# A two-dimensional convolution with Toeplitz blocks, followed by a score-weighted sum: X in two layouts, and the second convolution with the Toeplitz blocks as weights

## The chip, the cores and the metric

The kernel runs on one core of one Trainium2 chip. The metric is device time in microseconds (us) of one execution, the median of several runs. A profile is one further execution, recorded by the hardware profiler; its times are us from the start of its span. The engines are named as the profile does: PE (TensorE matmuls), PEld (TensorE weight loads), DVE (VectorE), ACT (ScalarE), POOL (GpSimd) and SP (SyncE, which here only issues DMAs).

## What is computed

The input x has 4 images, 64 channels, 256 x 256 pixels, in f32. Two layers follow each other. Cut to what matters:

```python
# layer 0: per channel c, a causal 2-D convolution with a separable kernel, and a bias
hx, hy = implicit_filter(X...), implicit_filter(Y...)      # [256, 64] each, three small sine layers
k = hx[:, None, :] * hy[None, :, :]                        # per channel an outer product
y = irfft2(rfft2(x, 512) * rfft2(k, 512) / 512)[..., :256, :256]
x = y + x * bias[:, None, None]
# layer 1: per image and channel
scores = einsum('bpsd,bptd->bpst', x, x) / sqrt(256)
red = sum(scores * weights, axis=-1, keepdims=True)        # weights: [64, 256, 256]
x = batch_norm(x + red)                                    # mean and variance per channel
```

As the kernel k is an outer product, the convolution of a channel is two one-dimensional convolutions, each a product with a lower triangular Toeplitz matrix of 256 x 256: `y = Tx X Ty'`.

## The kernel before

**Channels.** Everything is done channel by channel, 64 of them, four images (two pairs v and u) at a time. The 128 partitions hold two halves of 64 rows, so all products are 64 x 64 tiles, and four of them (t = 0 to 3: two halves of the input partitions, two of the output partitions) stand in the program one after the other. I call such four a group. Each f32 product leaves two matmul records and two weight loads in the trace.

**The products of one channel**, with the columns that each group moves:

- The first convolution, `z_slots` (line 263), in two halves m = 0, 1 of 8 groups: 256, 128, 64, 64 columns and the same again. Blocks of X are the weights, Toeplitz blocks move. A part that two output blocks share is made once from the sums `xs` (`sums`, line 225, on DVE) by `shared_slots` (line 234): 4 groups of 64 columns; ACT copies it to `kept` (line 243). ACT and DVE bring the result to SBUF as z (`copy_z`, line 272; `add_shared`, line 278).
- The second convolution, `x0_slots` (line 329), in two halves m of 8 groups: 256, 192, 128, 64 columns and the same again. Blocks of z are the weights, Toeplitz blocks move. `add_bias` (line 350) takes each half out of PSUM on DVE, adds bias times x from `xt`, and writes x0.
- The scores, `gram` (line 398), in two halves v of 8 groups: four of 192 columns and four of 128. DVE multiplies them with the weights (`weigh_pair`: lines 435 and 424).

That is 52 groups and 7,424 columns for a channel: 2,560 in the second convolution, 2,048 in the first, 256 shared, 2,560 for the scores.

**The rest of layer 1.** POOL adds the weighted scores over partitions (`all_sum`, line 489), DVE adds the sum to x0 (`add_red`, line 505), ACT squares and writes the normalised output (`squares`, line 558; `finish`, line 622).

**Order.** The order on each engine is written out by hand in the loop over channels. Iteration c does the second convolution of channel c, the first convolution of channel c + 1, the scores of channel c, and later steps of channels c - 1 to c - 4. On PE: `x0_slots(c, m=0)` with two `shared` groups; `x0_slots(c, m=1)` alternating with `z_slots(c+1, m=0)`; `z_slots(c+1, m=1)`; `gram(c, 0)`; `gram(c, 1)` with the first two `shared` groups of channel c + 2. On DVE: `add_bias` m=0, `sums(c+2)`, `add_red` of channel c - 2 first half, `add_bias` m=1, `add_red` second half, `add_shared` twice, then the eight small products and two large ones of `weigh_pair`, twice.

**PSUM.** One pool `ps` of 4 tiles, two banks each, filled in turn; a tile is reused when the fourth one before it has been read.

**DMAs.** SP issues, for each channel, four loads of `xt` (256 KB each, channel c + 3), four of the Toeplitz tile `toep` (16 of its 64 partitions each, channel c + 3) and four stores `out`. ACT issues the load of the weights `w` and a small store `rows`. `toep` is copied to the other 64 partitions by ACT (`copy_h`, line 208). Channel 0 has its own order: `first_x0` (line 366) does the first two blocks of both halves before the last two.

Of the kernel before, what the change touches and what calls it, by code (L numbers as in the profile page):

```python
# [16 lines left out]
P = 128  # L17
EMB = 33
FFT = 2 * S
H = P // 2  # L20
# [21 lines left out]
def conv_scores_bn_kernel(  # L42
    ctx: ExitStack,
    tc: tile.TileContext,
    xT: bass.AP,
    wl: bass.AP,
    zw: bass.AP,
# [21 lines left out]

    xts, ws, hs = {}, {}, {}  # L70

    def load_xt(c, v, n):
        if c not in xts:
            xts[c] = ld.tile([P, 2, 4, S], F32, tag="xt", name=f"xt_{c}", bufs=4)
        part = bass.ts(n, 2)
        nc.sync.dma_start(xts[c][:, v, part], xT[c, v, :, part])

    PARTS = ((0, 0), (1, 0), (0, 1), (1, 1))
# [28 lines left out]
    for part in PARTS:  # L107
        load_xt(0, *part)
    eye_sb = const.tile([P, P], F32, name="eye_sb")
# [4 lines left out]
    for part in PARTS:  # L114
        load_xt(1, *part)
    g_sb = const.tile([P, 2 * S + H], F32, name="g_sb")
# [99 lines left out]
    def pair_of_banks(name):  # L216
        return ps.tile([P, 2, 2, S], F32, tag="ps", name=name)
# [4 lines left out]
    def sums(c):  # L222

        xss[c] = wk.tile([P, 2, S], F32, tag="xs", name=f"xs_{c}")
        nc.vector.tensor_tensor(xss[c], xts[c][:, :, 1], xts[c][:, :, 2], ALU.add)

# [21 lines left out]
    def z_slots(c, m, p1):  # L248


        toep = hs[c].rearrange("p (b s) -> p b s", s=H)
        for k in range(2):
            for i, (cols, outs) in enumerate((
                (slice(9, 13), slice(0, 4)),
                (slice(5, 13, 7), slice(0, 3, 2)),
                (slice(7, 8), slice(1, 2)),
                (slice(12, 13), slice(0, 1)),
            )):
                for t in range(4):
                    u, v = t % 2, t // 2  # L260
                    rows = bass.ts(u, H)
                    out = p1[bass.ts(v, H), u, k].rearrange("p (b s) -> p b s", s=H)
                    nc.tensor.matmul(  # L263
                        out[:, outs], lhsT=xts[c][rows, v, i, bass.ts(2 * m + k, H)],
                        rhs=toep[rows, cols], start=(i == 0), stop=(i == 3),
                    )
                yield

    def copy_z(c, m, p1):
        z = zs[c][:, m].rearrange("p u k s -> p (u k) s")  # L270
        y = p1.rearrange("p u k s -> p (u k) s")
        nc.scalar.copy(z[:, :, :P], y[:, :, : P - 1 : -1])  # L272

    def add_shared(c, m, p1):
        z = zs[c][:, m].rearrange("p u k (b s) -> p (u k) b s", s=H)
        y = p1.rearrange("p u k (b s) -> p (u k) b s", s=H)
        part = kept[c][:, m].rearrange("p u (k s) -> p (u k) s", s=H)
        nc.vector.tensor_tensor(  # L278
            z[:, :, :1:-1, ::-1], y[:, :, :2],
            part[:, :, None, :].to_broadcast([P, 4, 2, H]), ALU.add,  # L280
        )

    def plain_slots(c, m, p1):


        toep = hs[c][:, PLAIN:]
        for k in range(2):
            for i in range(4):
                for t in range(4):
                    u, v = t % 2, t // 2  # L290
                    rows = bass.ts(u, H)
                    nc.tensor.matmul(  # L292
                        p1[bass.ts(v, H), u, k, : S - H * i],
                        lhsT=xts[c][rows, v, i, bass.ts(2 * m + k, H)],
                        rhs=toep[rows, H * i : S], start=(i == 0), stop=(i == 3),
                    )
                yield
# [6 lines left out]
    def take(*slots):  # L304

        slots = list(slots)
        while slots:
            slots = [s for s in slots if next(s, s) is None]

    def take_with(slots, between):  # L310

        for n, _ in enumerate(slots):
            if n % 4 == 3:
                next(between, None)

    def copy_z_plain(c, m, p1):
        for u in range(2):
            nc.scalar.copy(zs[c][:, m, u], p1[:, u, :, ::-1])

    def x0_slots(c, z, m, p2):  # L320


        toep = hs[c]
        for i in range(2):
            for k in range(4):
                for t in range(4):
                    v, u = t % 2, t // 2
                    rows = bass.ts(v, H)
                    nc.tensor.matmul(  # L329
                        p2[bass.ts(u, H), v, i, : S - H * k],  # L330
                        lhsT=z[rows, k // 2, u, k % 2, bass.ts(2 * m + i, H)],
                        rhs=toep[rows, H * k : S], start=(k == 0), stop=(k == 3),
                    )
                yield

# [5 lines left out]
    def add_bias(c, m, p2, split=False):  # L341
        part = bass.ts(m, 2)
        if split:
            for v in range(2):
                nc.vector.scalar_tensor_tensor(  # L345
                    st8[c][0][:, v, part], xts[c][:, v, part], chan_sb[:, 0, c : c + 1],
                    p2[:, v, :, ::-1], ALU.mult, ALU.add,
                )
            return
        nc.vector.scalar_tensor_tensor(  # L350
            st8[c][0][:, :, part], xts[c][:, :, part], chan_sb[:, 0, c : c + 1],
            p2[:, :, :, ::-1], ALU.mult, ALU.add,
        )

    def first_x0(z):

        toep = hs[0]
        p2 = [pair_of_banks(f"p2_0_{m}") for m in range(2)]
        for half in range(2):
            for m in range(2):  # L360
                for i in range(2):
                    for k in range(2 * half, 2 * half + 2):
                        for t in range(4):
                            v, u = t % 2, t // 2
                            rows = bass.ts(v, H)
                            nc.tensor.matmul(
                                p2[m][bass.ts(u, H), v, i, : S - H * k],
                                lhsT=z[rows, k // 2, u, k % 2, bass.ts(2 * m + i, H)],
                                rhs=toep[rows, H * k : S],
                                start=(i == 0 and k == 0), stop=(i == 1 and k == 3),  # L370
                            )
                if half:
                    add_bias(0, m, p2[m], split=True)

# [432 lines left out]
    for part in PARTS:  # L807
        load_xt(2, *part)
    for n in range(4):
# [4 lines left out]
    def begin_z(c):  # L814
        zs[c] = wk.tile([P, 2, 2, 2, S], F32, tag="z", name=f"z_{c}")

# [20 lines left out]
    for c in range(C - 2):  # L837
# [5 lines left out]
        if f >= 0:  # L843
            tot = sum_squares(f, moms[f])
        parts_of(c, 0)
        if c + 3 < C:
            load_xt(c + 3, 0, 0)
        if c:
            p2 = pair_of_banks(f"p2_{c}_0")
            take_with(x0_slots(c, z, 0, p2), shared)  # L850
            if short:
                keep_shared(c + 1, both)
            keep_rows(p)
            load_w(c + 1, nc.scalar)
            add_rows(p)
            add_bias(c, 0, p2)
        else:
            load_w(c + 1)
            first_x0(z)
        if q >= 0:  # L860
# [4 lines left out]
        else:  # L865
            steps = iter(())
        parts_of(c, 1)
        if c + 3 < C:
            load_xt(c + 3, 1, 0)
            for n in range(2):  # L870
                load_h(c + 3, n)
# [5 lines left out]
        next(steps, None)  # L877
        slots = []
        if c:
            p2 = pair_of_banks(f"p2_{c}_1")  # L880
            slots.append(x0_slots(c, z, 1, p2))
        p1 = [pair_of_banks(f"p1_{c + 1}_0")]
        slots.append((z_slots if short else plain_slots)(c + 1, 0, p1[0]))
        take(*slots)
        copy_any = copy_z if short else copy_z_plain
        copy_any(c + 1, 0, p1[0])
        if c:
            add_bias(c, 1, p2)
        next(steps, None)
        parts_of(c, 2)  # L890
        if c + 3 < C:
            load_xt(c + 3, 0, 1)
            for n in range(2, 4):
                load_h(c + 3, n)
# [15 lines left out]
        if q >= 0:  # L910
            minus_mean(moms[q])
            squares(q, moms[q], 0)
        parts_of(c, 3)
        if c + 3 < C:
            load_xt(c + 3, 1, 1)
        if q >= 0:
            squares(q, moms[q], 1)
        parts_of(c, 4)
        gram(c, 0)
        shared = iter(())  # L920
        if c + 2 < C - 1:
            both = ps.tile([P, 2, 8, H], F32, tag="ps", name=f"shared_{c + 2}")
            shared = shared_slots(c + 2, both)
        gs = gram_banks(c, 1)
        take_with(gram_slots(c, 1, gs), shared)
        weigh_pair(c, 1, gs)
    last_channels(C - 1)
# [71 lines left out]
```

## Time and profile before

| | before |
|---|---|
| median of 3 runs | 900.13 us (898.49 to 902.55) |
| the profiled execution | 892.19 us, of which its span is 890.4 us |
| granted TensorE clock, mean over the span | 0.993 |
| PE, PEld, DVE, ACT, POOL busy | 96%, 90%, 81%, 70%, 54% |
| matmul records | 26,626, and as many weight loads |
| DMA | 175.56 MB, mean 197 GB/s |

A busy PE in this table is matmul records laid side by side; four tiles run at once, so a record's length is not the time that it takes from the others. In the groups of instructions, `L329 PE MATMUL p<-toep,z 64*64 64x256` is a matmul of line 329, 64 x 64 weights, 256 columns moved, which writes a PSUM tile p from toep and z; `xCOUNT` stands after it, then busy us, and the mean ns of one.

### The profile page before, as it was taken

The page shows a single profiled execution, that of the slowest core. Times are in us where ns is not written, and L with a number is a line of the kernel's source. Part 1 is how long each engine was busy: PE and PEld are TensorE (multiplying, and loading weights), DVE is VectorE, ACT ScalarE, POOL GpSimd, SP SyncE. Part 2 cuts the span into 40 slices and gives each one's busy share as a digit, 9 for nine tenths or more (in the row PEclk, how much of TensorE's full clock was granted, in tenths as well). Part 3 has the DMA queues.
Part 4 walks back from the last instruction along what each step waited for, and adds up shares of the span by engine and source line. Part 5 has one row for each costly group of instructions (what it writes and reads, how often), then busy time and mean ns, then how long its engine had stood idle before and what let it go on. Part 6 is the DMA issues. An engine that isn't in the chain of part 4 may idle for free.

```text
span 890.4 us, 59137 instructions
## 1 busy us (share of the span) xinstructions
PE 857.6 (96%) x26626; PEld 800.0 (90%) x26626; DVE 721.2 (81%) x2160; ACT 621.9 (70%) x1157; POOL 480.8 (54%) x255
## 2 busy tenths in 40 slices
PE   7999999999999998999999999999999999999994
PEld 5899999899899897989899899898999899998984
DVE  3478888888788787888788888888788788888887
ACT  2237778677677676767778677667677668767687
POOL 0065565566465565565565565565565566566440
PEclk9999999999999999999999999999999999999997
DMA  6634666666566665666666666666666666666535
GB/s 194 212 123 135 215 210 209 199 210 208 190 193 219 196 216 184 205 208 197 209 199 211 208 195 198 212 204 202 193 216 197 197 214 196 226 204 200 169 125 191
DMA packets 103545, 175.56 MB, mean 197 GB/s; under 512 B 24219, under 2 KB 25148, under 8 KB 103292
## 3 DMA queue, kind: packets, MB, share of 16 engines
q1 hardware_dynamic: 80188, 149.66, 49.9%
q10 hardware_dynamic: 18224, 21.85, 8.3%
q8 instruction: 209, 3.42, 1.6%
q0 software_dynamic: 4880, 0.27, 0.7%
q14 instruction: 44, 0.36, 0.1%
HBM read 102.56 MB, written 69.03 MB: 193 GB/s over the span
## 4 chain that ended last, share of the span: by engine, by line
PE 90%; DVE 3%; issue 2%; DMA 2%; ACT 1%; POOL 1%; SPq 0%; ACTq 0%; DVEq 0%
PE g L398 31%; PE p L329 30%; PE p L263 25%; PE shared L234 3%; DMA g_dram<-g_sb 1%; PE p L292 1%; POOL rd L489 1%; DVE junk L435 0%; DMA fw_sb<-in_fw 0%; DMA toep<-g_dram 0%; DVE x L505 0%; DVE x L345 0%; DMA xt<-in_xT 0%; DVE x L547 0%; ACT o L622 0%
## 5 line engine op out<-in xcount | busy, mean ns | idle before, releaser
L329 PE MATMUL p<-toep,z 64*64 64x64 f32 (+3 forms) x8064 | 400.9, 297 | 4.1 <-issue 4.1
L489 POOL PARTITION_ALL_REDUCE rd<-pr x61 | 375.9, 6162 | 26.5 <-DMA pr<-rows 26.3
L263 PE MATMUL p<-toep,xt 64*64 64x64 f32 (+2 forms) x7808 | 337.2, 271 | 6.6 <-issue 6.2
L329 PEld LDWEIGHTS p<-toep,z 64*64 64x64 f32 x8064 | 324.0, 133 | 20.2 <-issue 8.3
L398 PE MATMUL g<-x 64*64 64x128 f32 (+1 forms) x8192 | 311.2, 297 | 3.3 <-issue 2.1
L263 PEld LDWEIGHTS p<-toep,xt 64*64 64x64 f32 x7808 | 284.4, 133 | 27.0 <-issue 12.3
L398 PEld LDWEIGHTS g<-x 64*64 64x64 f32 x8192 | 278.4, 133 | 16.3 <-issue 7.5
L350 DVE SCALAR_TENSOR_TENSOR x<-xt,chan_sb,p 128x1024 f32<-128x1024 f32 x122 | 156.2, 1280 | 77.8 <-PE p L329 77.6
L622 ACT ACTIVATE o<-x,sh,g 128x512 f32<-128x512 f32 x252 | 201.7, 803 | 0.3 <-DVE sh L610 0.3
L435 DVE SCALAR_TENSOR_TENSOR junk<-g,w 128x192 f32<-128x192 f32 x512 | 152.4, 354 | 48.8 <-PE g L398 48.0
L479 POOL DMA_DIRECT2D pr<-rows x61 | 54.2, 888 | 217.0 <-DMA rows<-across 139.7
L505 DVE SCALAR_TENSOR_TENSOR x<-x,rd 128x1024 f32<-128x1024 f32 x122 | 148.6, 1219 | 7.0 <-ACT rd L498 6.8
L558 ACT ACTIVATE sq<-x,mom 128x1024 f32<-128x1024 f32 x127 | 145.0, 1142 | 2.1
L243 ACT COPY kept<-shared 128x512 f32<-128x512 f32 x61 | 35.8, 586 | 116.4 <-PE shared L234 116.4
L234 PE MATMUL shared<-toep,xs 64*64 64x64 f32 x1952 | 106.2, 218 | 0.2 <-issue 0.2
L272 ACT COPY z<-p 128x512 f32<-128x512 f32 x122 | 71.4, 586 | 44.3 <-PE p L263 43.0
L511 POOL PARTITION_ALL_REDUCE mom<-mom x62 | 24.2, 391 | 139.9 <-DVE x L505 137.0
L234 PEld LDWEIGHTS shared<-toep,xs 64*64 64x64 f32 x1952 | 92.2, 134 | 1.5 <-issue 0.4
L424 DVE SCALAR_TENSOR_TENSOR pr<-g,w 128x512 f32<-128x512 f32 x126 | 84.2, 668 | 0.0
L278 DVE TENSOR_TENSOR z<-p,kept 128x512 f32<-128x512 f32 x122 | 83.1, 682 | 0.8 <-ACT z L272 0.8
L208 ACT COPY toep<-toep 64x832 f32<-64x832 f32 x63 | 55.7, 884 | 12.8 <-DMA toep<-g_dram 11.4
L498 ACT COPY rd<-rd 64x512 f32<-64x512 f32 (+1 forms) x62 | 38.0, 613 | 32.7 <-POOL tot L564 8.4
(100 smaller groups left out, 442.2 us busy)
## 6 DMA issues: line engine op xcount, KB each, us to landing
xt<-in_xT SPq DMA_DIRECT2D x256, 256.0 KB
out<-o SPq DMA_DIRECT2D x256, 256.0 KB
w<-in_wl ACTq DMA_DIRECT2D x61, 320.0 KB
toep<-g_dram SPq DMA_DIRECT2D x252, 52.0 KB
rows<-across ACTq DMA_DIRECT2D x61, 16.0 KB
pr<-rows POOLq DMA_DIRECT2D x61, 4.0 KB, 3.3
w<-in_wl SPq DMA_DIRECT2D x3, 320.0 KB
g_dram<-g_sb ACTq DMA_DIRECT2D x1, 576.0 KB
```

What stands on the lines that cost most here:

```text
L234: nc.tensor.matmul(both[bass.ts(v, H), u, k], lhsT=xss[c][rows, v, bass.ts(k, H)], rhs=toep[rows, 11], start=(k == 0), stop=(k == 3),)
L263: nc.tensor.matmul(out[:, outs], lhsT=xts[c][rows, v, i, bass.ts(2 * m + k, H)], rhs=toep[rows, cols], start=(i == 0), stop=(i == 3),)
L278: nc.vector.tensor_tensor(z[:, :, :1:-1, ::-1], y[:, :, :2], part[:, :, None, :].to_broadcast([P, 4, 2, H]), ALU.add,)
L329: nc.tensor.matmul(p2[bass.ts(u, H), v, i, : S - H * k], lhsT=z[rows, k // 2, u, k % 2, bass.ts(2 * m + i, H)], rhs=toep[rows, H * k : S], ...
L350: nc.vector.scalar_tensor_tensor(st8[c][0][:, :, part], xts[c][:, :, part], chan_sb[:, 0, c : c + 1], p2[:, :, :, ::-1], ALU.mult, ALU.add,)
L398: nc.tensor.matmul(gs[bass.ts(h, H), u, o, :], lhsT=xb[rows, v, i, m, :], rhs=xb[rows, v, i, t, :], start=(i == 0), stop=(i == 3),)
L424: nc.vector.scalar_tensor_tensor(pr[:, 2 * v : 2 * v + 2].rearrange("p u (t s) -> p u t s", s=H), both[:, :, COL, :], 1.0 / math.sqrt(S), ...
L435: nc.vector.scalar_tensor_tensor(junk, g[:, part, :], 1.0 / math.sqrt(S), w[:, 3 * n : 3 * n + 3, :], ALU.mult, ALU.mult, accum_out=red0[: ...
L489: nc.gpsimd.partition_all_reduce(rd[:, part].rearrange("p b s -> p (b s)"), sp[:, part].rearrange("p b s -> p (b s)"), P, RED.add,)
L505: nc.vector.scalar_tensor_tensor(x0[:, v], x0[:, v], 1.0, rd[:, 2 * v, None, :].to_broadcast([P, 4, S]), ALU.mult, ALU.add, accum_out=moms ...
L558: nc.scalar.activation(sq, st8[c][0][:, v], AF.Square, bias=mom[:, 5:6], accum_out=mom[:, 6 + v : 7 + v])
L622: nc.scalar.activation(o, y, AF.Identity, bias=sh, scale=g)
```

## The change

X comes to the chip a second time. `xR` holds it with rows on the partitions, `xT` with columns (and now in reversed order of columns). `xr`, loaded from `xR`, feeds the first convolution and `sums`, so the rows are convolved first; `xt` is only read by `add_bias`. The host swaps the two filters accordingly and reverses one axis of the output again.

In the second convolution weights and moving operand are exchanged: a Toeplitz block of 64 columns is the weight, and z moves, two blocks of 256 columns in one product where two are due. Its groups become 512 and 256 columns for m=0, and 512, 512, 512 and 256 for m=1. To make this possible z is stored as `[P, 4, 2, S]`, and its result comes out of PSUM in forward order.

In the loop the four `shared` groups of channel c + 1 now all stand in `x0_slots(c, m=0)`, two after each of its groups, and two `z_slots` groups stand after each of the four groups of `x0_slots(c, m=1)`. `gram(c, 1)` stands alone. The PSUM tile of `shared` is therefore taken second in the iteration, not before the last. SP issues four more loads a channel: `xt` of channel c + 2 and `xr` of channel c + 3, from 3 buffers each. `first_x0` is gone, and channel 0 is done like the others.

```diff
+    def load_xr(c, v, n):
+        if c not in xrs:
+            xrs[c] = ld.tile([P, 2, 4, S], F32, tag="xr", name=f"xr_{c}", bufs=3)
+        part = bass.ts(n, 2)
+        nc.sync.dma_start(xrs[c][:, v, part], xR[c, v, :, part])
...
     def take_with(slots, between):
 
-        for n, _ in enumerate(slots):
-            if n % 4 == 3:
+        for _ in slots:
+            for _ in range(2):
                 next(between, None)
...
         toep = hs[c]
-        for i in range(2):
-            for k in range(4):
-                for t in range(4):
-                    v, u = t % 2, t // 2
-                    rows = bass.ts(v, H)
-                    nc.tensor.matmul(
-                        p2[bass.ts(u, H), v, i, : S - H * k],
-                        lhsT=z[rows, k // 2, u, k % 2, bass.ts(2 * m + i, H)],
-                        rhs=toep[rows, H * k : S], start=(k == 0), stop=(k == 3),
-                    )
-                yield
+        products = [(0, 2 * m, 2)]
+        if m:
+            products += [(1, 1, 2), (2, 0, 2)]
+        products += [(2 * m + 1, 0, 1)]
+        for k, i, n in products:
+            for t in range(4):
+                v, u = t % 2, t // 2
+                rows = bass.ts(v, H)
+                nc.tensor.matmul(
+                    p2[bass.ts(u, H), v, 2 - n :], lhsT=toep[rows, S - H * (k + 1) :][:, :H],
+                    rhs=z[rows, i : i + n, u], start=(k == 0), stop=(n == 1),
+                )
+            yield
...
-        if c:
-            p2 = pair_of_banks(f"p2_{c}_0")
-            take_with(x0_slots(c, z, 0, p2), shared)
-            if short:
-                keep_shared(c + 1, both)
+        p2 = pair_of_banks(f"p2_{c}_0")
+        shared = iter(())
+        if short:
+            both = ps.tile([P, 2, 8, H], F32, tag="ps", name=f"shared_{c + 1}")
+            shared = shared_slots(c + 1, both)
+        take_with(x0_slots(c, z, 0, p2), shared)
+        if short:
+            keep_shared(c + 1, both)
...
-        slots = []
-        if c:
-            p2 = pair_of_banks(f"p2_{c}_1")
-            slots.append(x0_slots(c, z, 1, p2))
+        p2 = pair_of_banks(f"p2_{c}_1")
         p1 = [pair_of_banks(f"p1_{c + 1}_0")]
-        slots.append((z_slots if short else plain_slots)(c + 1, 0, p1[0]))
-        take(*slots)
+        take_with(x0_slots(c, z, 1, p2), (z_slots if short else plain_slots)(c + 1, 0, p1[0]))
...
+        if c + 2 < C:
+            load_xt(c + 2, 1, 1)
         if c + 3 < C:
-            load_xt(c + 3, 1, 1)
+            load_xr(c + 3, 1, 1)
...
         gram(c, 0)
-        shared = iter(())
-        if c + 2 < C - 1:
-            both = ps.tile([P, 2, 8, H], F32, tag="ps", name=f"shared_{c + 2}")
-            shared = shared_slots(c + 2, both)
-        gs = gram_banks(c, 1)
-        take_with(gram_slots(c, 1, gs), shared)
-        weigh_pair(c, 1, gs)
+        gram(c, 1)
```

At the start SP now loads `xr` of channel 0, the constants, `w`, `xt` of channel 0 and `xr` of channel 1, then the Toeplitz tiles with `xt` of channel 1 and `xr` of channel 2 between them: 2 MB (eight loads of 256 KB) more than before, half of it ahead of the first Toeplitz tile.

## The prediction

> **What bounds the kernel now.** First the busy times and the chain that ended last, to see which engine sets the end.
>
> ```profile
> PE 857.6 (96%) x26626; PEld 800.0 (90%) x26626; DVE 721.2 (81%) x2160; ACT 621.9 (70%) x1157; POOL 480.8 (54%) x255
> PE 90%; DVE 3%; issue 2%; DMA 2%; ACT 1%; POOL 1%; SPq 0%; ACTq 0%; DVEq 0%
> ```
>
> PE has 90% of the chain, so I ask what a channel costs on PE. The chain in order of time shows where each channel's score products begin (start, length):
>
> ```profile
> 46.18 3.42 PE g L398 x85
> ...
> 111.19 3.42 PE g L398 x90
> 123.90 3.42 PE g L398 x90
> 136.61 3.42 PE g L398 x89
> 149.32 3.70 PE g L398 x88
> ...
> 818.01 3.48 PE g L398 x96
> ```
>
> Clean channels follow each other at 12.71 us. From 46.18 to 818.01 lie 58 channels, 13.31 us each. So 0.60 us a channel is lost, 36 us over 61 channels. What is a clean channel made of? Groups of instructions by form, line 329 (behind the first bar: busy us in all, ns of one record):
>
> ```profile
> L329 PE MATMUL p<-toep,z 64*64 64x256 f32 x2016 | 189.5, 379 | 1.0 <-issue 1.0
> L329 PE MATMUL p<-toep,z 64*64 64x64 f32 x2016 | 107.9, 218 | 1.3 <-issue 1.3
> ```
>
> 192 more columns cost 161 ns, 0.839 ns a column and record; two records each, so 7,424 columns need 12.45 us. Only 0.26 us of a clean channel is the price of having 52 groups: 5 ns a group.
>
> And the 0.60 us? I went to one late channel; chain in order of time, 173 to 178 us:
>
> ```profile
> 174.46 0.55 PE p L263 x16
> 175.01 0.92 issue
> 175.93 1.56 PE p L263 x56
> ```
>
> PE waits 0.92 us for nothing that the profile names. In the waits, too, PEld's largest are "issue" (28 us before lines 263, 329 and 398); none for data reaches 4 us in all. The DMA queues show what it is:
>
> ```profile
> q1 hardware_dynamic: 80188, 149.66, 49.9%
> q10 hardware_dynamic: 18224, 21.85, 8.3%
> q8 instruction: 209, 3.42, 1.6%
> ```
>
> q8 moves instructions: 209 packets of 16 KB for 53,252 matmul and weight-load instructions, a block of 256 each. In the packet records every PE gap over 0.25 us between 50 and 840 us falls on the same place of the count of PE instructions modulo 256, about 1.3 us after the block's packet ended. So PE runs out of instructions. From the moment it passes one block's border, the next packet starts 1.33 us later on average, takes 1.10 us (1.6% of 16 engines over the span, by 209), and is usable 1.3 us after that: 3.9 us (5% to 95%: 3.1 to 4.7 us, after 150 us). A block lasts 16 groups: 16 x 12.71 / 52 = 3.91 us. Every other block is late. Setting those latencies against the windows that the order of groups gives, the mean shortfall is 0.17 us a block, 3.25 blocks a channel: 0.56 us, against 0.60 seen. I take this as the cause.
>
> [...]
>
> **The change, part by part,** against the profiled execution's 892.19 us.
>
> *Fewer groups.* 16 groups of the second convolution become 6, with the same 2,560 columns; the program falls from 13,313 to 10,753 matmuls. 10 x 5 ns x 62 channels = -3 us. No row has 512 columns; the records from 64 to 256 columns lie on one line, so I take the line. It could gain nothing or cost a few ns: 0 to -5 us.
>
> *Fewer blocks.* 43,012 instructions are 168 blocks, 2.63 a channel. A block now lasts 16 x 12.66 / 42 = 4.82 us on average, though 8 groups of the first convolution followed by 8 of 192 score columns still last under 3.9. With the latency unchanged the shortfall is 0.05 us a block, 0.13 a channel.
>
> *More loads.* 256 x 256 KB = 67.1 MB. By q1's row (49.9% for 149.66 MB) that is 22 points: the 16 engines go from 60 to 83% busy. A block's packet must find its turn there. Packets asked for while 40 to 60% of the engines were busy in the next us started 1.1 us later, at 80% and more 1.6 us, with single means up to 1.8. I add 0.4 us to the latency (from 0 to 1.0): shortfall 0.13 us a block, 0.35 a channel (0.39 and 1.02 at +1.0). Scaled by 0.60 / 0.56 that is 0.37 instead of 0.60: 0.23 x 61 = -14 us; between -28 us at +0 and +25 us at +1.0.
>
> *SP's queue.* An `xt` issue takes 0.65 us, four more a channel 2.6 us; SP issues 6.5 us of 13.3 now and waits 379 us in all for ACT's outputs, so it has room. But at the fourth place `xr` stands behind `out` and `xt`: 0.45 us of issue and 0.75 us of transfer (256 KB at the 355 GB/s of stretches with all engines busy) later than `xt` today. `sums` on DVE needs it. Today `xs` starts 1.67 us (median) after the last packet and never earlier than 0.63 us, so about 1.0 is spare:
>
> ```profile
> DVE xs L225 <- DMA xt<-in_xT: 8.7, 12, 2.0
> DVE x L350 <- PE p L329: 77.6, 113, 2.4
> DVE junk L435 <- PE g L398: 48.0, 88, 5.9
> ```
>
> 0.2 us of new wait, and as `add_bias` can start 0.4 us sooner (m=0 has 768 columns, not 1,280), 0.6. Behind it in DVE's order stand `add_red`, then `add_bias` m=1, which waits for PE anyhow: the last two rows are 126 us of DVE waiting for PE, 2 us a channel. Priced at nothing under that cover; bare, it is 0.6 x 61 = 37 us.
>
> *PSUM.* With `shared` taken second, the first half of z for channel c + 1 takes the tile of `gram(c-1, 1)`. From the timeline, second convolution's start and last read of that tile:
>
> ```profile
> 409.73 0.39 PE L329 MATMUL p<-toep,z 64*64 64x256 f32 x3
> 411.46 0.65 DVE L424 SCALAR_TENSOR_TENSOR pr<-g,w 128x512 f32<-128x512 f32 x1
> ```
>
> The read ends 2.4 us after; PE comes to it after 768 + 256 + 512 columns, 2.6 us. Zero, but bare only by 0.2 us: 0.1 us late would be 6 us. `add_bias`, `copy_z` and `add_shared` keep their sizes; reversed and forward reads differ by nothing in the rows (1,280 ns for line 350 reversed, 1,219 for line 505 forward, which sums besides), so zero, with 60 ns x 122 = -7 us of DVE at most, off the path. The loads use buffers that an earlier iteration has read; one load of `w` goes from SP to ACT.
>
> *Start.* 1 MB more ahead of the first Toeplitz tile and the store g_dram (14.16 to 20.41 us in the chain, then the load of toep, then PE at 27.19): 1 MB at 355 GB/s is 3 us. The DMA is 0.66 busy before 30 us, so part may hide; the second extra MB delays channel 2's tile. +3 us, 0 to +6. Losing `first_x0` costs nothing: m=0 now needs only z's first half.
>
> Sum: 892.2 - 3 - 14 + 3 = 878 us. The median of the runs lies 7.9 us above the profiled execution; so 886.
>
> **The rivals.**
>
> *The fetching engine fills up (slower).* Each packet of q8 runs on one DMA engine, and if it is always the same, that engine does per channel 96 packets of 2 KB x 96 ns = 9.2, 8 of `w` x 130 ns = 1.0, 2.63 blocks x 1.10 = 2.9, small ones 0.4: 13.5 us by mean durations. That is above 13.31, and loads, `sums` and PE would follow it: 13.5 x 61 against 13.31 is +12, +3 at the start: 907, median 915. By medians (84, 102, 1009 ns) it is 11.9 and doesn't bind; it decides from about 13 us. For it: durations stretch when all engines are busy. Against: before, the same sum is 11.1 of 13.3 and `xs` rarely waits.
>
> *The fetch slows by what the change saves (no change).* At +0.7 us of latency the shortfall is 0.64 a channel, as now: 892 - 3 + 3, median 900.
>
> *The latency stays (more gain).* 892.2 - 3 - 28 + 0 = 861, median 869. For it: packets started after 0.6 us, not 1.5, between 100 and 150 us, at the same DMA share.
>
> *The late `xr`* loses its cover, when its packets queue a us longer: half of 37 us on top of the sum is 896, median 904.
>
> **How the numbers follow.** Forecast 0.42 (own range 876 to 894), fetching engine 0.22, slowed fetch 0.16, unchanged latency 0.12, late `xr` 0.08. A run of this kernel can tell 0.5% from no change, 895.6 to 904.6. Faster: nearly all of the forecast and the unchanged latency, 0.51. Same: most of the slowed fetch, 0.15. Slower 0.34. Range 868 to 914: it leaves out about half of the fetching engine and a little below.
>
> **What would show it.** Right: q8 near 170 packets; line 340 with 512 columns near 379 + 256 x 0.839 = 594 ns; clean channels at 12.65 us; a mean channel near 13.0; PE's issue waits down by a third or more; DMA near 280 GB/s; the score products of channel 0 some 3 us later. Wrong: PE waiting for `xs`, `g` or `xr`; `xs` waiting in most channels; channels of 13.5 us with DMA flat at 9; 512 columns well off the line.

## The result, and the profile after

The changed kernel takes 934.50 us, the median of 4 runs (929.13 to 941.93), where before takes 900.03. The ratio is 1.0386, with an interval of 1.0308 to 1.0463: slower, by 35 us. The profiled execution took 929.13 us, its span 927.4, at a mean granted clock of 0.983 (0.993 before). The clock is not the loss: clean channels take 12.64 us in the changed kernel, and 12.64 in `one_layout` (below), at 0.992.

The page of the changed kernel, busy times and then shares of the chain that ended last:

```profile
PE 862.1 (93%) x21506; PEld 676.6 (73%) x21506; DVE 706.6 (76%) x2158; ACT 614.0 (66%) x1157; POOL 481.3 (52%) x255
DMA 34%; DVE 15%; PE 12%; POOL 11%; ACT 11%; issue 8%; SPq 8%; ACTq 0%; DVEq 0%; POOLq 0%
```

PE is still busy for 93% of the span, but its share of the chain fell from 90% to 12%. A busy time doesn't say who sets the end. One group of instructions by form (busy us, ns of one), and three DMA queues (packets, MB, share of 16 engines):

```profile
L340 PE MATMUL p<-z,toep 64*64 64x512 f32 x2048 | 279.0, 590 | 0.0
q1 hardware_dynamic: 116908, 216.46, 70.2%
q10 hardware_dynamic: 18368, 22.18, 7.5%
q8 instruction: 169, 2.77, 1.3%
```

The 512 columns cost what the line through the shorter products said (590 ns, 594 by the line), and there are 40 instruction blocks fewer (169 packets of q8, 209 before). A clean channel takes 12.64 us, the mean of 58 channels is 13.85 (13.31 before). The waits of the changed kernel say where that goes (first a line of the page, with DVE's idle time before `sums` behind the last bar; then us in all, times, longest):

```profile
L234 DVE TENSOR_TENSOR xs<-xr 128x512 f32<-128x512 f32 x61 | 42.4, 694 | 153.6 <-DMA xr<-in_xR 101.5
DVE xs L234 <- DMA xr<-in_xR: 101.5, 36, 4.8
DVE x L354 <- PE p L340: 11.9, 5, 8.3
DVE x L489 <- ACT rd L482: 14.3, 8, 6.7
POOL rd L473 <- DMA pr<-rows: 65.7, 43, 4.1
PEld g L382 <- DVE x L354: 45.9, 34, 4.1
PE g L382 <- DVE x L354: 34.0, 29, 3.7
```

The scores now wait for `add_bias`, which stands on DVE behind `add_red` and `sums`, and `sums` waits for `xr`. PE's gaps of over 0.1 us between matmul records from 50 to 840 us, counted in the trace, are 40 us: 32 before scores and 8 at borders of instruction blocks (one place of the count of PE instructions, the sequencer's included, modulo 256). Before, they were 13 us, all at block borders. All gaps below are counted in this way.

### The profile page after: what moved, and what is told of

The parts are those of the page before. It is cut to its first block, busy times and chain, and to the rows that moved or that the text cites. A ratio compares the mean times of both kernels' runs of the same rounds, so it can differ in the third digit from the quotient of the medians.

```text
span 927.4 us, 49216 instructions
## 1 busy us (share of the span) xinstructions
PE 862.1 (93%) x21506; PEld 676.6 (73%) x21506; DVE 706.6 (76%) x2158; ACT 614.0 (66%) x1157; POOL 481.3 (52%) x255
## 4 chain that ended last, share of the span: by engine, by line
DMA 34%; DVE 15%; PE 12%; POOL 11%; ACT 11%; issue 8%; SPq 8%; ACTq 0%; DVEq 0%; POOLq 0%
DMA xr<-in_xR 12%; POOL rd L473 10%; DMA pr<-rows 7%; DVE x L489 7%; PE g L382 6%; DMA toep<-g_dram 4%; DMA rows<-across 4%; PE p L340 3%; ACT sq L542 3%; ACT o L606 3%; DMA w<-in_wl 3%; SPq L77 3%; PE p L272 2%; DMA out<-o 2%; SPq L212 2%
## 5 line engine op out<-in xcount | busy, mean ns | idle before, releaser
L340 PE MATMUL p<-z,toep 64*64 64x512 f32 (+1 forms) x3072 | 359.9, 519 | 0.1
L382 PE MATMUL g<-x 64*64 64x192 f32 (+1 forms) x8192 | 311.9, 301 | 39.2 <-DVE x L354 34.0
L272 PEld LDWEIGHTS p<-toep,xr 64*64 64x64 f32 x7808 | 252.6, 134 | 119.9 <-issue 53.5
L272 PE MATMUL p<-toep,xr 64*64 64x64 f32 (+2 forms) x7808 | 276.3, 271 | 5.6 <-issue 3.0
L354 DVE SCALAR_TENSOR_TENSOR x<-xt,chan_sb,p 128x1024 f32<-128x1024 f32 (+1 forms) x132 | 162.8, 1236 | 11.9 <-PE p L340 11.9
L489 DVE SCALAR_TENSOR_TENSOR x<-x,rd 128x1024 f32<-128x1024 f32 x122 | 148.6, 1218 | 14.4 <-ACT rd L482 14.3
L234 DVE TENSOR_TENSOR xs<-xr 128x512 f32<-128x512 f32 x61 | 42.4, 694 | 153.6 <-DMA xr<-in_xR 101.5
L340 PEld LDWEIGHTS p<-z,toep 64*64 64x64 f32 x3072 | 113.3, 134 | 7.1 <-issue 5.4
L243 PEld LDWEIGHTS shared<-toep,xs 64*64 64x64 f32 x1952 | 62.4, 134 | 33.7 <-issue 16.8
L537 ACT ACTIVATE mom<-mom 128x1 f32<-128x1 f32 x62 | 18.3, 295 | 73.7 <-POOL mom L495 72.6
```

The source lines that it names most:

```text
L272: nc.tensor.matmul(out[:, outs], lhsT=xrs[c][rows, v, i, bass.ts(2 * m + k, H)], rhs=toep[rows, cols], start=(i == 0), stop=(i == 3),)
L340: nc.tensor.matmul(p2[bass.ts(u, H), v, 2 - n :], lhsT=toep[rows, S - H * (k + 1) :][:, :H], rhs=z[rows, i : i + n, u], start=(k == 0), st ...
L354: nc.vector.scalar_tensor_tensor(st8[c][0][:, v, part], xts[c][:, v, part], chan_sb[:, 0, c : c + 1], p2[:, v], ALU.mult, ALU.add,)
L382: nc.tensor.matmul(gs[bass.ts(h, H), u, o, :], lhsT=xb[rows, v, i, m, :], rhs=xb[rows, v, i, t, :], start=(i == 0), stop=(i == 3),)
L489: nc.vector.scalar_tensor_tensor(x0[:, v], x0[:, v], 1.0, rd[:, 2 * v, None, :].to_broadcast([P, 4, S]), ALU.mult, ALU.add, accum_out=moms ...
```

## The experiments

**Which part of the change costs?** The exchange without the second load, and the second load without the exchange.

```diff
 # one_layout: the changed kernel without the loads of xt, four buffers for xr
-                st8[c][0][:, v, part], xts[c][:, v, part], chan_sb[:, 0, c : c + 1],
+                st8[c][0][:, v, part], xrs[c][:, v, part], chan_sb[:, 0, c : c + 1],
 # before_twice_loaded: the kernel before, behind each load of xt
+        nc.sync.dma_start(xes[c][:, v, part], xT[c, v, :, part])
```

> The changed kernel without the loads of xt: add_bias reads xr instead (so bias times x is that of transposed pixels; the output differs from the reference's in that), with 4 buffers of xr. The exchange of operands, the fewer matmuls and the order are the changed kernel's, the bytes are those of before. If the loss comes from the second load in any way (theories 1 and 2) the time falls below that of before: by the prediction's terms for unchanged block latency, 892 - 3 - 28 = 861 profiled, 869 median (860 to 880). If the instruction blocks are not what PE waited for before, only the 3 us of fewer groups remain: 895 to 900. Theory 3, the exchange costs: above 925.

> The kernel before with each xt load issued a second time into a tile that nothing reads (two buffers), behind the first. The first load of each place is 0.45 us of issue later than its turn, the bytes are those of the changed kernel, the matmuls those of before (208 instruction blocks). If the block latency grows with the load as the prediction has it (+0.4 us), the shortfall rises from 0.17 to 0.42 us a block, 0.8 us a channel: 950 (at +0.2 us: 922). If the second load costs only where sums waits for it (theory 1 alone), 900 to 910. Theory 2, full DMA engines: above 930, with loads late and DVE waiting for xt.

`one_layout`: 857.96 us, ratio 0.9414 [0.9360, 0.9468]. `before_twice_loaded`: 998.08 us, 1.0957 [1.0899, 1.1015]. So the load costs 9.6% on the kernel before and 10.3% (1.0386 / 0.9414) on the exchanged one, and the exchange alone saves 5 to 6% in either. The median of before itself moved between 898 and 908 us from one series of runs to another, so a figure that crosses series, as 10.3% does (934.50 / 857.96 is 8.9%), is good to about 1%. The two kernels with the load pay for it in different places. The chain's shares of `one_layout`, then those of `before_twice_loaded` and its waits of PE for nothing that the profile names:

```profile
PE 89%; DVE 4%; DMA 3%; ACT 1%; POOL 1%; issue 1%; SPq 1%; DVEq 0%; ACTq 0%
```

```profile
PE 85%; issue 9%; DVE 3%; DMA 2%; SPq 1%; ACT 0%; DVEq 0%; ACTq 0%
```

```profile
PE p L266 <- issue: 42.3, 43, 2.3
PE p L332 <- issue: 19.4, 31, 1.5
PE g L401 <- issue: 14.5, 27, 1.1
```

In the second, all 103 gaps, 72 us, lie at block borders, where before has 13 us: what PE waits for there is instruction blocks that come late. (Its scores of channel 0 also begin at 40.1 us and not 33.0.) In `one_layout`, with 169 blocks and nearly the DMA rate of before (204 GB/s, 197), the gaps are 2 us in all, none at a border, and the mean channel takes 12.71 us.

**Does the second load cost by its bytes, or because `add_bias` waits for it?**

```diff
 # one_layout_unread: all loads of the changed kernel, xt read by nothing (two buffers for xt,
 # four for xr)
-                st8[c][0][:, v, part], xts[c][:, v, part], chan_sb[:, 0, c : c + 1],
+                st8[c][0][:, v, part], xrs[c][:, v, part], chan_sb[:, 0, c : c + 1],
```

> The changed kernel with all its loads, but add_bias reads xr instead of xt, so that the bias is added from the wrong layout and nothing reads or waits for xt. Loop theory: the bytes alone lengthen the DMAs inside the loop, so the time is that of the changed kernel, 915 to 945. Rival, that add_bias waits for the late second load: 858 to 875, the time without that load.

941.55 us, 1.0375 [1.0298, 1.0452], the changed kernel's ratio. The loads do it with nothing waiting for `xt`. Whether by their bytes or by their issues, which stand on SP ahead of those of `xr`, this run doesn't separate.

**Is it the late `xr`?** Two ways to give `sums` its data in time:

```diff
 # sums_later: behind add_bias m=1 on DVE
-        if c + 2 < C - 1:
-            sums(c + 2)
         if q >= 0:
             add_red(q, 0)
...
         add_bias(c, 1, p2)
...
+        if c + 2 < C - 1:
+            sums(c + 2)
 # xr_earlier: each load one place earlier in SP's order (at the last place: c + 4)
-            load_xr(c + 3, 1, 1)
+            load_xr(c + 4, 0, 0)
```

> The changed kernel with one DVE instruction per channel moved: the sums of channel c + 2 stand behind add_bias of m=1 instead of ahead of add_red's first half, so the last xr load has about 4 us more. Theory 1, late xr: the 34 us are lost because sums waits in DVE's order for the last quarter of xr, which stands behind out and xt in SP's queue, and the scores wait for add_bias behind it; then the wait ahead of xs (154 us) nearly vanishes, the scores' wait for add_bias too, and the time falls to 900 +- 10. Theory 2, full DMA engines: the load as such is too much, every transfer is late; then the wait turns up elsewhere and the time stays above 925. Theory 3, the exchange of operands or the order of PSUM tiles costs the time: above 930.

> The changed kernel with every load of xr issued one place (about 3.3 us) earlier, in the buffers that there are: the last quarter of channel c + 3 at the third place of iteration c, and the first quarter of channel c + 4 at the fourth. DVE's order is as in the changed kernel. Theory 1, late xr: 900 +- 10, the wait ahead of xs under 40 us. Theory 2, full DMA engines: above 925, the bytes are the same. Theory 3: above 930.

933.62 us, 1.0273 [1.0201, 1.0344], and 943.39 us, 1.0358 [1.0300, 1.0417]. The first may have gained a point by its ratio (none in us), the second nothing. The waits moved instead of going; `sums_later`:

```profile
DVE x L489 <- ACT rd L482: 184.3, 60, 7.8
...
POOL rd L473 <- DMA pr<-rows: 104.2, 44, 4.1
ACT rd L482 <- POOL rd L473: 101.2, 28, 9.5
```

DVE now stands before `add_red` and waits for POOL's sum. Following that wait back gives a loop of two channels, the **rows loop**: `add_red` of channel k holds up `add_bias`, the scores and the row sums of channel k + 2 on DVE; ACT stores those (`rows`), POOL issues the DMA that adds them to `pr`, waits for it, does `all_sum`, ACT copies half of `rd`, and only then can `add_red` of k + 2 start. Mean us of each step, from the instructions' times between 100 and 820 us:

| step | before | one_layout | changed | xr_earlier | rows_first_xr_earlier |
|---|---|---|---|---|---|
| row sums (L453) to issue of `rows` | 1.19 | 0.33 | 0.88 | 2.18 | 0.21 |
| to issue of `pr` | 3.67 | 4.39 | 4.89 | 5.45 | 4.58 |
| to its landing | 3.41 | 3.63 | 4.35 | 4.08 | 4.77 |
| to `all_sum` | 0.46 | 0.39 | 0.33 | 0.27 | 0.20 |
| `all_sum` | 6.16 | 6.15 | 6.14 | 6.13 | 6.13 |
| to ACT's copy, and the copy | 1.32 | 0.68 | 1.08 | 1.19 | 0.82 |
| to `add_red` | 0.20 | 0.47 | 1.21 | 0.04 | 0.03 |
| `add_red` to row sums of k + 2 | 10.28 | 9.39 | 8.68 | 8.89 | 9.53 |
| half of the sum | 13.34 | 12.71 | 13.78 | 14.12 | 13.16 |

The sum is two channels in any kernel; what tells is where the loop waits for something outside of it. In `xr_earlier` and `sums_later` `add_red` waits for ACT's copy in nearly every channel (57 and 60 times, 103 and 184 us): there the rows loop decides. In the changed kernel it does so 8 times. From the row sums' store to the landing of `pr` it takes 9.2 us there, 1.2 more than in `one_layout`.

But there is a second loop, of one channel, the **xr loop**. The chain of the changed kernel in order of time (start, length), from one second half of `add_red` to the next (SP issues a store in L607 and a load of `xt` in L77):

```profile
769.69 1.15 DVE x L489 x2
...
770.93 0.40 POOL mom L495
...
771.36 0.30 ACT mom L537
...
773.16 0.72 ACT o L606
...
773.89 0.34 SPq L607
...
774.28 0.43 SPq L77
...
774.76 4.46 DMA xr<-in_xR
...
779.40 0.16 DVE xs L234
...
780.01 1.23 DVE x L489 x2
...
782.68 1.15 DVE x L489 x2
```

13.0 us, above PE's 12.64: `add_red` lets ACT finish an output, whose store stands on SP ahead of the loads, `xr` takes 4.46 us, and `sums`, `add_red`, `add_bias` follow on DVE. From 100 to 820 us the trace has 53 such rounds. In every one DVE stands before `sums`, 2.6 us on average (the waits above put a part down to others than `xr`). In 31 the store goes out 0.03 us after its output is there, as here, and a round takes 13.2 us on average. In 22 SP is still issuing earlier loads, the store is 1.0 us late, and a round takes 14.6 us; in 12 of these the loads had stood behind an output that follows ACT's copy of `rd`, which had waited for `all_sum`: so the rows loop also feeds the xr loop. Against `one_layout`, from the store to the issue of `xr` it is 0.6 us more (the issue of `xt` stands between), the store is 0.4 us later, and the load itself 0.8 us longer: 1.8 us a round. Taking the late `xr` away leaves the rows loop.

**Does the chain through `all_sum` bind without any more DMA?**

```diff
 # one_layout_longer_sum
             all_sum(p)
+            all_sum(p, slice(0, 2))
```

> The kernel with one layout (no second load, 858 us), and all_sum of the first two images done a second time with the same result, which adds about 3 us of POOL (half of 6.1) inside the loop and no byte of DMA. POOL is busy for about half of the span. Loop theory: in that kernel the loop of two channels takes 25.4 us with about 1.2 to 2.2 us of waiting in it, so 3 us more make 0.4 to 0.9 us a channel: 885 to 915, without any more DMA. Full-engines theory, and any in which the loop has room: within 1% of 858.

965.39 us, 1.0630 [1.0581, 1.0679]: 12.9% over `one_layout`, twice what was expected, on a POOL that is busy for 70%. The chain in order of time:

```profile
466.09 1.15 DVE x L487 x2
...
467.74 6.11 POOL rd L471
...
473.93 3.24 POOL rd L471
...
477.19 0.61 ACT rd L480
...
480.51 1.14 DVE x L487 x2
```

14.4 us a channel, again from one second half of `add_red` to the next, this time through POOL and ACT. Without the extra 3.24 us it is 11.2, 1.4 under PE's 12.64. So the order written by hand holds several loops, all little longer or shorter than PE's channel. That is a loop of one channel, not the one of two that the expectation had in mind. `sums` took 1.7 us instead of 0.7 there (last section), but `add_red` behind it waited for ACT's copy in all 61 channels, so that is not where the excess comes from.

**Shortening the rows loop.** First by moving `add_red` on DVE:

```diff
 # reds_later, on sums_later (reds_and_rows: also keep_rows at the start of an iteration)
-            add_red(q, 0)
         next(steps, None)
...
-        if q >= 0:
-            add_red(q, 1)
-            sum_means(moms[q])
-        if p >= 0:
-            all_sum(p)
...
                 add_shared(c + 1, m, p1[m])
...
+        if q >= 0:
+            add_red(q, 0)
+            add_red(q, 1)
+            sum_means(moms[q])
+        if p >= 0:
+            all_sum(p)
 # red_behind_bias, on sums_later (red_behind_bias_rows: also keep_rows at the start;
 # before_red_behind_bias: the same two moves in the kernel before)
-            add_red(q, 0)
         next(steps, None)
...
         add_bias(c, 1, p2)
...
             sums(c + 2)
         if q >= 0:
+            add_red(q, 0)
             add_red(q, 1)
```

> The changed kernel with the same loads; on DVE, sums(c+2) moves behind add_bias m=1 and both halves of add_red of channel c-2 move behind add_shared, just before the products of weigh_pair, with sum_means and all_sum behind them on POOL. Loop theory: add_red of channel k holds up add_bias, the scores and the row sums of channel k+2, whose two DMAs and all_sum hold up add_red of k+2. In the profile of the changed kernel that loop takes 27.6 us for two channels, 13.8 each: 0.9 to the issue of rows, 4.9 to the issue of pr, 4.4 to its landing, 0.3, all_sum 6.1, 0.5, 0.6 for ACT's copy, 1.2, and 8.7 from add_red to the next row sums. The move takes add_bias, add_shared and half of the waits (3 to 4 us) out of it, so it can turn in 12 us a channel, and PE decides again, with the instruction blocks' loss: 870 to 890. Full-engines theory: bytes set the pace whatever the order, 920 to 940. Late-xr theory (only the waits of sums): that was taken away alone and gave nothing, so 930.

> As the kernel with add_red later, and ACT issues the store rows at the start of an iteration, ahead of the outputs of channel c-4 and of keep_shared. Loop theory: another 0.3 to 0.9 us of slack in a loop that no longer decides, so the same time within 1%, 865 to 890; if it is clearly faster than the kernel without it, the loop still decided there. Full-engines theory: 920 to 940.

> The changed kernel with the same loads; on DVE, sums(c+2) and the first half of add_red of channel c-2 move behind add_bias m=1, so that DVE does add_bias, add_bias, sums, add_red, add_red, add_shared. With add_red later still, behind add_shared, a loop of one channel had closed (add_red, mom, all_sum 6.2 us, ACT's copy of rd, and behind it on ACT copy_z, for which add_shared waits: 14.7 us a channel); here nothing that add_red waits for stands behind copy_z. Loop theory: in the changed kernel the loop of two channels takes 27.6 us; the move takes 1.4 us of add_bias and the waits of PE and sums out of it, leaves 23 to 26, 11.7 to 13.1 a channel: 870 to 905. Full-engines theory: 920 to 940.

> As the kernel with add_red behind add_bias, and ACT issues the store rows at the start of an iteration, ahead of an output and of keep_shared. If the loop of two channels still decides there, the issue 0.5 to 1 us sooner makes it 0.2 to 0.5 us a channel, 1.5 to 3%, faster than without; if PE decides, no difference.

> The kernel before with the same two moves on DVE. Its loop of two channels holds 2.5 us of waiting for others than itself, and PE loses its 36 us to instruction blocks: no change, ratio 0.99 to 1.01. If that loop decided there too, 2 to 4% faster.

| kernel | us | ratio to before |
|---|---|---|
| reds_later | 1007.67 | 1.1092 [1.1032, 1.1152] |
| reds_and_rows | 1016.13 | 1.1183 [1.1125, 1.1242] |
| red_behind_bias | 933.68 | 1.0347 [1.0278, 1.0415] |
| red_behind_bias_rows | 926.83 | 1.0266 [1.0223, 1.0309] |
| before_red_behind_bias | 926.31 | 1.0264 [1.0222, 1.0305] |

None came near the times expected of the rows loop, and the store `rows` issued sooner changed under 1% either way. `reds_later` closed a loop of its own: `all_sum` behind `add_red` on POOL, ACT's copy of `rd` ahead of `copy_z` on ACT, `add_shared` waiting for `copy_z`, and `add_red` behind it, 14.7 us. `red_behind_bias_rows` runs at 13.7 us a channel with PE waiting 0.8 us in each before `z_slots`, until 0.1 us after the last product of `weigh_pair`, whose PSUM tile it takes: `sums` and both halves of `add_red` had moved into DVE's busiest stretch. These kernels say that moves on DVE have no room, and nothing for or against the rows loop.

Then with DVE's order left alone:

```diff
 # rows_first (and before_rows_first): ACT issues rows at the start of an iteration
+        if p >= 0:
+            keep_rows(p)
         parts_of(c, 0)
...
             keep_shared(c + 1, both)
-        if p >= 0:
-            keep_rows(p)
 # rows_first_xr_earlier: rows_first and xr_earlier
```

> The changed kernel with its own order on DVE; only the issue of the store rows moves, to the start of an iteration on ACT, ahead of an output of channel c-4 and of keep_shared. Loop theory: in the changed kernel the loop of two channels takes 27.6 us, 0.9 of it from the row sums to the issue of rows and 4.9 from there to the issue of pr; where rows stood first (with add_red behind add_bias) they were 0.03 and 3.9. 1.8 us less is 0.9 us a channel: 875 to 905, with xs still waiting for xr now and then. Theory that the waits of xs for xr decide: no change, 925 to 940.

> As the kernel with rows first, and each load of xr one place earlier in SP's order, which alone gave nothing (1.0358): there the loop took 28.2 us, with 2.2 us before the issue of rows and 5.5 behind it. Loop theory: both waits go, 28.2 - 2.2 - 1.6 = 24.4 us for two channels, under PE's 12.64 each; PE decides again and loses only to instruction blocks (11 to 20 us): 865 to 890, faster than before. If DVE or POOL close another loop: 900 to 930.

> The kernel before with rows issued first in the same way. Loop theory: there PE decides, and waits for instruction blocks, not for the loop: ratio 0.99 to 1.01.

`rows_first`: 915.11 us, 1.0159 [1.0066, 1.0253]. `rows_first_xr_earlier`: 899.67 us, 0.9986 [0.9951, 1.0020], the time of before, with all of the 67 MB. `xr_earlier` alone had given nothing; with the rows loop shortened as well it is worth almost 2%. Its chain is PE's again:

```profile
PE 61%; DMA 17%; DVE 6%; ACT 5%; POOL 4%; issue 3%; SPq 2%; ACTq 0%; DVEq 0%; POOLq 0%
```

`before_rows_first` was expected to stay and took 933.60 us, 1.0355 [1.0281, 1.0430]. Its bytes are those of before, and its loss shows at instruction blocks: 47 us of gaps at borders against 13, in the waits

```profile
PE p L263 <- issue: 33.0, 30, 1.7
PE g L398 <- issue: 9.7, 16, 2.3
```

where before has 6.2 and 2.1 us. `before_red_behind_bias` has 31 us at borders. A block's packet starts 1.76 us after PE passes the last border, on average, against 1.44 before (150 to 840 us). So what the blocks cost changes with the order alone; that it is the moment at which the data moves is a reading, not shown.

**Two last tries at the loop.**

```diff
 # split_sum, split_sum_rows_xr (on rows_first_xr_earlier), before_split_sum
-            all_sum(p)
+            all_sum(p, slice(0, 2))
+            all_sum(p, slice(2, 4))
...
-            pick_red(q)
+            pick_red(q, 0)
...
         copy_h(c + 2)
+            pick_red(q, 1)
 # rows_unread: all_sum doesn't wait for the DMAs of the row sums
-            pr[0:1].rearrange("p b (n q i) -> p (b n) q i", n=2, i=32),
+            spare[0:1].rearrange("p b (n q i) -> p (b n) q i", n=2, i=32),
...
-            add_rows(p)
         add_bias(c, 0, p2)
...
             all_sum(p)
+            add_rows(p)
```

> The changed kernel, one edit: all_sum on POOL in two calls of two images each, and ACT copies each half of rd when it is there, so that add_red of the first half needs only the first call. No byte of DMA less. A second call on two images had cost about 3.3 us, the whole 6.1. Loop theory: 6.1 + 0.6 become 3.3 + 0.4 in the loop of 27.6 us for two channels, 24.5, 12.3 a channel: 880 to 910 with the waits of xs left. Full-engines theory and late-xr theory: 925 to 945.

> The kernel with rows first and xr earlier (0.9986 of before; its loop takes 26.3 us for two channels, PE's clean channel 12.64) with all_sum in two halves. Loop theory: 26.3 - 3.0 = 23.3 us, 11.7 a channel, so PE decides, and loses 11 to 20 us to instruction blocks: 865 to 885, ratio 0.96 to 0.985, faster than both kernels. If POOL's second half holds up sums (some sums that started while all_sum ran took 2 to 4 us instead of 0.7), the gain is lost: 890 to 905.

> The kernel before with all_sum in two halves. PE decides there and waits for instruction blocks: 0.99 to 1.01 by the loop theory. The two other edits that moved its order, with the same bytes, cost it 2.6 and 3.6%, all as waits for instruction blocks, so that a slower result of that kind is possible; faster than 0.99 would speak for the loop there too.

> The changed kernel with all its loads, stores and DMAs, but the store rows is added into a tile that nothing reads, behind all_sum on POOL, so that all_sum does not wait for the two DMAs (the part of the row sums is missing from the result). Loop theory: those two DMAs and the waits before them, 10.4 of the 27.6 us for two channels, leave the loop; what is left of it, and the loop of one channel (add_red, mom, all_sum, copy, add_red, add_bias: about 11 us), lies under PE's 12.64: 865 to 890, with instruction blocks the main loss, though the second load stays. If the late xr holds sums all the same: 900 to 915. Full-engines theory: 925 to 945.

`split_sum` 939.96 us, 1.0464 [1.0393, 1.0534]; `split_sum_rows_xr` 909.08 us, 1.0111 [1.0050, 1.0172]; `before_split_sum` 897.16 us, 0.9985 [0.9946, 1.0024]. The halves gained nothing: the copy of the second half stood on ACT behind `root`, which waits for a sum that stands on POOL behind the second call (74.7 us of waiting in `split_sum`).

`rows_unread`: 911.95 us, 1.0134 [1.0061, 1.0207]. Taking the two DMAs out of the rows loop is worth 2.5% and not the 5 to 7% that the rows loop as the only cause asked for; the time falls into the range given for the late `xr`. Its waits:

```profile
DVE xs L236 <- DMA xr<-in_xR: 94.8, 32, 5.4
```

## Why the prediction was wrong

886 us were predicted, 934.5 measured, above the top of the range (914).

**What held.** The products: 594 ns forecast and 590 measured, a clean channel 12.65 and 12.64, 170 blocks and 169; DMA ran at 261 GB/s instead of 280, as the same bytes took longer. The theory of the instruction blocks: `before_twice_loaded` has 72 us of gaps, all at the borders. And the exchange itself: the case without a longer latency was 892.2 - 3 - 28 = 861 us, and `one_layout`, where no load is added and no block is late (2 us of gaps, none at a border), took 859.2 profiled. That this is so close is in part luck: in its own series before took 908 us, and the ratio 0.9414 is a gain of 50 us, not 33.

**The blocks** in the changed kernel also went as forecast. From the border passed to the end of the next block's packet it takes 2.94 us on average against 2.53 before, 0.41 more where 0.4 was put (150 to 840 us; the prediction's 1.33 us to the start of the packet do not add up to its 3.9, but counted in this way they are 1.49 behind 150 us, and the 3.9 comes out). The gaps at borders fell from 13 to 8 us, and PE's waits for "issue" by a third ("down by a third or more"), before and then changed:

```profile
PE p L263 <- issue: 6.2, 15, 1.0
PE p L329 <- issue: 4.1, 8, 0.8
PE g L398 <- issue: 2.1, 5, 0.6
```

```profile
PE g L382 <- issue: 4.8, 7, 1.5
PE p L272 <- issue: 3.0, 6, 0.8
```

That the size came out was not to be relied on: three reorderings of the kernel before with its own bytes have 19, 31 and 47 us of gaps at borders where it has 13. (In the term's range the end at +1.0 us is not scaled like the others; scaled it is +30 us, not +25.) "The fetching engine fills up" is not what happened: 32 of the 40 us of gaps are at DVE's waits, not at the borders; that one engine has all of q8's packets was its assumption, and no row shows it.

**What failed: the term of the second load.** It was put at 0.4 us on the fetch latency, 14 us, and 3 us at the start: from 861 to 878. Between the profiled runs of `one_layout` and the changed kernel it is 70 us, from 859 to 929; a mean channel goes from 12.71 to 13.85 us, which over 61 channels is the same 70. Two of its steps went wrong.

- "Priced at nothing under that cover; bare, it is 37 us." The wait of `sums` for `xr` was foreseen, and its cover was read from before: 126 us in which DVE waits for PE. That cover exists because PE sets the end. The wait stands in a loop that comes back to itself through ACT, SP's queue and the next `xr`; once such a loop is longer than PE's channel, DVE no longer waits for PE (12 us of `add_bias` waiting for PE in the changed kernel, 78 before), and the cover is gone as a whole. The wait was also too small: 0.6 us a channel forecast, 153.6 us in all or 2.5 a channel measured. Its 0.4 us for the earlier `add_bias` come out only if one of a column's two records is counted: from the iteration's first product to the last of m=0 there are 448 columns less (896 instead of 1,344, with `shared`), by the prediction's own price 0.75 us, so bare it should have been 58 us. The rival "late `xr`" had the right place at a chance of 0.08, at half of its bare price, and it too would have been 30 us short.
- The rows loop was not in the sum at all. Its DMAs are small (16 and 4 KB), so they were not counted among what the load touches, but they take longer: `pr` from issue to landing takes 3.41, 3.63, 3.88 and 4.35 us on average at 197, 204, 244 and 261 GB/s (before, `one_layout`, `before_twice_loaded`, changed). The rate alone does not set it: `before_rows_first` has 4.45 us with the bytes of before, `reds_later` 5.35 at 240 GB/s.

**The start.** 3 us were right in size only. The scores of channel 0 begin at 35.9 us against 33.0, but in `one_layout`, which loads less, at 36.0: the extra MB is not needed for it. What is left is the loss of `first_x0`, which had been put at nothing; no run took that back alone, and in the other runs of the changed kernel's kind these scores begin anywhere from 33.5 to 36.2 us.

**PSUM.** Bare by 0.2 us was right: in 22 channels the first product of z starts 0.1 us after the read of that tile ends, and 0.3 us after its turn, 6 to 7 us that were put at zero.

**What stays open.** That the second load costs its time with nothing waiting for it is shown (`one_layout_unread`), and that shortening both loops brings the changed kernel level with before. How much comes by its bytes and how much by its issues on SP is only read from the trace: no run put the loads on another queue. Not tried was to take both loops away at once; the DMA engines' load may have a part of its own. Nor do the runs say whether the small DMAs wait in their queues or at the memory.

## What to carry to other kernels

The slack of an engine beside the bound is no cover for a wait that lies on a loop: follow the waiting instruction forward until it comes back to itself, add the loop's latencies, DMAs and queues included, and compare the sum per round with the bound's. Extra bytes on DMA engines 60% busy were not free here, though they fit: from `one_layout` to the changed kernel, 67 MB more went with a load of `xr` that takes 0.8 us longer in its loop, with 4.35 us instead of 3.63 for the small `pr`, and with 2.94 us instead of 2.26 from a border to the end of the next block's packet. In a hand-written order near its bound test an exchange and the load that it needs apart; here one was worth minus 5 to 6% and the other plus 9 to 10%.

## What the runs showed of the hardware

**DVE held up by POOL.** In `xr_earlier` `sums` is ready early and falls into `all_sum`:

```profile
L234 DVE TENSOR_TENSOR xs<-xr 128x512 f32<-128x512 f32 x61 | 88.4, 1449 | 29.0 <-DMA xr<-in_xR 21.7
```

Of the 61, the 13 outside of it and the 18 that start in its last 1.7 us take 0.69 us; the 30 that start in it before that take 2.24 on average, up to 4.6, and end 1.04 us before `all_sum` does. `add_bias`, with one operand in PSUM, takes no longer in `all_sum` than elsewhere: in the changed kernel the 59 of full size that start in it take 1.27 us, the other 65 take 1.26 (in `xr_earlier` all 124 take 1.27). `add_red`, with both in SBUF, took 2.7 us instead of 1.22 in six cases of `split_sum_rows_xr`. The long `sums` are over before the recorded end of `all_sum`, though POOL's spans are rough; what DVE and POOL contend for, no run shows.

**Instruction blocks and data.** PE's gaps at block borders went from 0 to 72 us over kernels with 169 or 209 blocks and 175 to 243 MB, and from 13 to 47 us at equal blocks and bytes, when ACT issued one 16 KB store sooner (`before_rows_first`). From the border to the end of the next block's packet it took 2.26 us in `one_layout`, 2.53 before, 2.86 in `before_rows_first`, 2.94 in the changed kernel and 3.14 in `before_twice_loaded`.
